# A cross network kernel: set-up reordered under manual scheduling, and chunk 0's h1 made while M is under way, its samples' halves side by side in the output columns

## The chip, the cores and the metric

One core of one Trainium2 chip. The time is the device time of one execution in microseconds (us); medians of several executions on the same chip are given. All arithmetic is fp32. A span is the profiled execution's length on the core, about 2 us shorter than that execution's time.

## The reference

A compressed interaction network of three layers on x of shape (1024, 64, 16): samples, fields, embedding.

```python
x0 = h = x
for i in range(3):                                   # each W: (128, 64 * fields of h)
    z = einsum('bfe,bge->bfge', x0, h).reshape(Bn, f0 * fh, e)
    y = einsum('oc,bce->boe', Ws[i], z) + bs[i][None, :, None]
    x_i, h = (y[:, :64], y[:, 64:]) if i != 2 else (y, y)
    xs.append(x_i)
return concatenate(xs, 1).sum(2) @ fc_w.T + fc_b     # (1024, 1)
```

What goes only into the last dot product can be folded into weights ahead of it. The kernel makes three 64 x 64 matrices: v0, v1 and v2, in which fc_w's parts are multiplied into W0, W1 and W2, and from v2 and W1 a tensor M. Per sample column, what remains is: h1 (64 weight columns from W0 against all products of two fields), p (64 columns from M and v1 against the same products), the products of h1 with p, and y = v0 x, times x, all summed.

## The kernel before

32 samples and 16 embedding places make a chunk of 512 columns; there are 32 chunks. Products of fields are made by VectorE in four pieces `z` a chunk (128 x 2048), TensorE contracts them against 17 tiles of `w_all`, 128 columns wide: 64 for h1, 64 for p. Every second chunk, `y` is made with the block-diagonal `bd` (v0 twice).

```python
zp = tc.tile_pool(name="zp", bufs=3)                 # z
ps = tc.tile_pool(name="ps", bufs=2, space=PSUM)
...
for k in range(32):                                  # v2: one column each
    nc.tensor.matmul(pv2[:, k:k+1], w2s[:, k, :], fc2, start=True, stop=True)
... # copies to v2t; pm = v2t x w1s -> m_sb (M); m_sb -> md (DRAM), five writes
... # md -> ms1, ms2 and w_all[0:64, NT, 64:128], skewed, eleven reads
... # rows v1, v0: 8 matmuls with fc01 (two columns), then DMA to w_all and bd

def products(c, j):
    z = zp.tile([128, NI, N], F32, tag="z", name="z")
    nc.vector.tensor_tensor(z, xas[c], xbs[c][:, j, :]..., ALU.mult)
    for i in range(NI):
        t = j * NI + i
        nc.tensor.matmul(accs[c], w_all[:, t, :], z[:, i, :], start=(t == 0), stop=False)

def combine(c):
    ... # q <- acc[64:128] (ScalarE); uu <- (acc[0:64] + bh1) * q (VectorE)
    if half == 0:
        return
    y = ps.tile([128, N], F32, tag="y", name=f"y_{c}", bufs=1)
    nc.tensor.matmul(y, bd, xxs[c // 2], start=True, stop=True)
    nc.vector.scalar_tensor_tensor(uu[:, 1, :], y, cx, xxs[c // 2], ALU.add, ALU.mult)
    nc.vector.tensor_reduce(acc[:, :, c // 2, :], uu..., AX.X, ALU.add)

for c in range(NCH + 1):
    if c + 1 < NCH: load_chunk(c + 1)
    if c < NCH:
        accs[c] = ...; products(c, 0); products(c, 1)
    if c > 0: combine(c - 1)
    if c < NCH:
        products(c, 2); products(c, 3); squares(c)
```

In this kernel the program order of the source is not the order that is built: a scheduler places instructions.

## Time and profile before

| | before |
|---|---|
| time, median (lowest to highest) | 552.89 us (551.77 to 554.76), 3 runs |
| profiled span (an execution of 556.77 us) | 555.0 us |
| set-up, until the first full matmul of chunk 0 | 66.3 us |
| a pair of chunks in the loop | 30.04 us |
| tail behind the last matmul of the loop | 8.7 us |

In the groups below (busy us, mean ns, then idle time before them), the main matmul never waits.

```profile
L236 PE MATMUL acc<-z,w_all 128*128 128x512 f32 x1024 | 447.2, 592 | 0.0
```

So only the set-up and the tail leave room.

### The profile page before, as it was taken

How to read it: one execution, taken by the hardware profiler on the slowest of the kernel's cores; microseconds unless marked ns; L12 is line 12 of the kernel's file. 1: busy time of each engine (PE TensorE's matmuls, PEld its weight loads, DVE VectorE, ACT ScalarE, POOL GpSimd, SP SyncE). 2: the span in 40 equal slices, each digit the busy share in tenths (PEclk: the TensorE clock that was granted, in tenths of full speed). 3: DMA queues.
4: the chain of work that ended last, by engine and by line, in shares of the span. 5: the costliest groups of instructions: out<-in, count | busy, mean ns of one | idle time of the engine just before them, and what ended most of it. 6: DMA issues, size and time to landing. Idle time of an engine off the chain costs nothing.

```text
span 555.0 us, 3402 instructions
## 1 busy us (share of the span) xinstructions
PE 515.9 (93%) x1240; PEld 231.9 (42%) x1240; DVE 352.0 (63%) x205; ACT 44.9 (8%) x81; POOL 5.3 (1%) x18
## 2 busy tenths in 40 slices
PE   5803799999999999999999999999999999999997
PEld 5600144444444444444444444444444444444442
DVE  0250076768677677768676867767776867686751
ACT  0100300000000000000000000000000000000001
POOL 3000000000000000000000000000000000000000
PEclk9967699999999999999999999999999999999999
DMA  8999998787777777877778777777787877874000
GB/s 254 185 283 210 205 208 170 144 163 146 156 153 159 150 152 162 180 161 161 160 147 165 146 154 154 154 150 154 161 180 161 165 155 151 162 152 77 0 1 0
DMA packets 33114, 85.33 MB, mean 154 GB/s; under 512 B 6405, under 2 KB 6949, under 8 KB 28710
## 3 DMA queue, kind: packets, MB, share of 16 engines
q1 hardware_dynamic: 29234, 81.84, 71.1%
q10 hardware_dynamic: 3608, 3.28, 2.8%
q8 instruction: 10, 0.16, 0.2%
q14 instruction: 6, 0.05, 0.0%
q0 software_dynamic: 256, 0.00, 0.0%
HBM read 82.89 MB, written 2.17 MB: 153 GB/s over the span
## 4 chain that ended last, share of the span: by engine, by line
PE 92%; DMA 6%; DVE 0%; ACT 0%; issue 0%; ACTq 0%; SPq 0%
PE acc L236 79%; PE acc L240 5%; DMA w<-in_wv 3%; PE pv L133 2%; PE y L254 2%; PE pv L197 2%; DMA ms<-md 1%; DMA fc<-in_fc_w 1%; DMA md<-m_sb 1%; PE pm L146 1%; PE po L281 0%; DVE acc L256 0%; DVE uu L255 0%; ACT res L289 0%; ACT q L249 0%
## 5 line engine op out<-in xcount | busy, mean ns | idle before, releaser
L236 PE MATMUL acc<-z,w_all 128*128 128x512 f32 x1024 | 447.2, 592 | 0.0
L231 DVE TENSOR_TENSOR z<-xa,xb 128x2048 f32<-128x2048 f32 x128 | 293.3, 2292 | 135.9 <-PE acc L236 134.6
L236 PEld LDWEIGHTS acc<-z,w_all 128*128 128x128 f32 x1024 | 194.5, 190 | 244.5 <-issue 244.4
L249 ACT COPY q<-acc 64x512 f32<-64x512 f32 x32 | 18.6, 582 | 443.8 <-PE acc L240 443.8
L197 PE MATMUL pv<-w,fc 128*2 128x512 f32 x16 | 11.5, 887 | 27.9 <-DMA w<-in_wv 14.9
L240 PE MATMUL acc<-zl,w_all 128*128 128x512 f32 x64 | 32.7, 592 | 0.0
L250 DVE SCALAR_TENSOR_TENSOR uu<-acc,bh,q 64x512 f32<-64x512 f32 x32 | 23.7, 740 | 10.0 <-ACT q L249 9.5
L239 ACT ACTIVATE zl<-xa 64x512 f32<-64x512 f32 x32 | 20.1, 628 | 3.6 <-DMA xa<-in_x 3.6
L133 PE MATMUL pv<-fc,w2s 128*128 128x1 f32 x64 | 13.8, 352 | 6.6 <-DMA fc<-in_fc_w 6.6
L256 DVE TENSOR_REDUCE acc<-uu 128x64 f32<-128x1024 f32 x16 | 19.5, 1220 | 0.5
L240 PEld LDWEIGHTS acc<-zl,w_all 128*128 128x128 f32 x64 | 12.2, 190 | 15.3 <-issue 15.3
L197 PEld LDWEIGHTS pv<-w,fc 128*2 128x2 f32 x16 | 1.6, 108 | 37.6 <-issue 21.5
L133 PEld LDWEIGHTS pv<-fc,w2s 128*128 128x128 f32 x64 | 13.7, 332 | 6.6 <-DMA fc<-in_fc_w 6.6
L254 PE MATMUL y<-xx,bd 128*128 128x512 f32 x32 | 16.3, 592 | 0.0
L136 DVE COPY v2t<-pv 64x32 f32<-64x32 f32 x2 | 0.4, 184 | 20.4 <-PE pv L133 20.4
L255 DVE SCALAR_TENSOR_TENSOR uu<-y,cx,xx 128x512 f32<-128x512 f32 x16 | 11.9, 745 | 0.0
L188 DVE TENSOR_TENSOR w_all<-ms,ms 128x1024 f32<-128x1024 f32 x1 | 1.2, 1224 | 13.2 <-DMA ms<-md 13.2
L254 PEld LDWEIGHTS y<-xx,bd 128*128 128x128 f32 x32 | 6.1, 190 | 7.7 <-issue 7.7
L199 ACT COPY vrow<-pv 2x512 f32<-2x512 f32 x8 | 4.2, 570 | 33.3 <-DMA ms<-md 32.2
L184 DVE MEMSET ms<- 64x64 f32 x1 | 0.1, 112 | 9.7 <-DMA ms<-md 9.7
L146 PE MATMUL pm<-w1s,v2t 64*64 64x512 f32 x16 | 5.6, 809 | 0.5 <-DVE v2t L137 0.5
L152 DVE COPY m_sb<-pm 64x512 f32<-64x512 f32 x4 | 2.7, 683 | 3.2 <-PE pm L146 3.2
(33 smaller groups left out, 21.0 us busy)
## 6 DMA issues: line engine op xcount, KB each, us to landing
xa<-in_x SPq DMA_DIRECT2D x64, 512.0 KB, 5.8
xb<-in_x SPq DMA_DIRECT2D x64, 512.0 KB, 7.1
zl<-in_x SPq DMA_DIRECT2D x32, 128.0 KB, 4.2
xx<-in_x SPq DMA_DIRECT2D x32, 128.0 KB, 4.1
w2s<-in_wv SPq DMA_DIRECT2D x4, 512.0 KB, 7.8
w<-in_wv SPq DMA_DIRECT2D x4, 512.0 KB, 11.9
w1s<-in_w1h SPq DMA_DIRECT2D x1, 1024.0 KB, 13.4
md<-m_sb ACTq DMA_DIRECT2D x2, 512.0 KB, 7.1
```

Source lines behind the costliest of these rows:

```text
L133: nc.tensor.matmul(pv2[:, k : k + 1], w2s[:, k, :], fc2, start=True, stop=True)
L146: nc.tensor.matmul(pm, v2t[to], w1s[to, m * 512 : (m + 1) * 512], start=True, stop=True)
L197: nc.tensor.matmul(pv, fc01, w01[:, m * 512 : (m + 1) * 512], start=True, stop=True)
L231: nc.vector.tensor_tensor(z, xas[c], xbs[c][:, j, :].unsqueeze(1).to_broadcast([128, NI, N]), ALU.mult)
L236: nc.tensor.matmul(accs[c], w_all[:, t, :], z[:, i, :], start=(t == 0), stop=False)
L239: nc.scalar.activation(zls[c][0:64], xas[c][0:64, 0, :], AF.Square)
L240: nc.tensor.matmul(accs[c], w_all[:, NT, :], zls[c], start=False, stop=True)
L249: nc.scalar.copy(q, accs[c][64:128])
L250: nc.vector.scalar_tensor_tensor(uu[to, 0, :], accs[c][0:64], bh1, q, ALU.add, ALU.mult)
L254: nc.tensor.matmul(y, bd, xxs[c // 2], start=True, stop=True)
L255: nc.vector.scalar_tensor_tensor(uu[:, 1, :], y, cx, xxs[c // 2], ALU.add, ALU.mult)
L256: nc.vector.tensor_reduce(acc[:, :, c // 2, :], uu.rearrange("p k (b e) -> p k b e", e=E), AX.X, ALU.add)
```

## The change

The intent: shorten the 66 us before the loop. Chunk 0's h1 (`ph`) needs only W0, so it can be made while M goes through DRAM; p (`pq`) follows when M is there. Each has 64 weight columns, half of the main matmul's 128, and one of 64 columns takes as long as one of 128. So the 512 samples are split: the first 256 go to output partitions 0 to 63 and the others to 64 to 127, two matmuls side by side. v2 is made as rows, v0 is postponed to chunk 2, and the writes of md are cut in seven. To hold the order the scheduler is turned off. The diff, cut to what matters:

```diff
+    ctx.enter_context(tc.manual_schedule())
-    zp = tc.tile_pool(name="zp", bufs=3)
+    zp = tc.tile_pool(name="zp", bufs=7)
-    ps = ... bufs=2
+    ps = ... bufs=4
 # v2
-    for k in range(32):
-        nc.tensor.matmul(pv2[:, k : k + 1], w2s[:, k, :], fc2, start=True, stop=True)
-    ... tensor_copy(v2t[to, ...], pv2[...])
+    for k in range(2):
+        for m in range(4):
+            nc.tensor.matmul(pv, fc2, w2s[k][:, cols], start=True, stop=True)
+            ... copy to vrow[0:1, cols], VectorE and ScalarE by turns
+        ... two nc.scalar.dma_start(out=v2t[...], in_=vrow[0:1, :]...)
 # md: seven writes; the last overlaps the sixth
+    nc.scalar.dma_start(out=md[64:96, 64:68, :], in_=m_lo[0:32, 0:4, :])
+    nc.scalar.dma_start(out=md[64:68, 64:96, :], in_=m_lo[0:4])
+    nc.scalar.copy(xas[0][F:128], xas[0][0:F])     # upper half of chunk 0
 # chunk 0
+    zs = [product(0, 0)]
+    first_weights()
+    zs += [product(0, j) for j in range(1, NJ)]
+    load_chunk(1)
+    def side_by_side(p, part, tiles):
+        cols = slice(part * F, (part + 1) * F)
+        for t in tiles:
+            for n in range(2):
+                nc.tensor.matmul(p[halves[n]], w_all[:, t, cols],
+                                 z[:, n * H2 : (n + 1) * H2], ...)
+    side_by_side(ph, 0, range(NT + 1))
+    second_weights()
+    constants()
+    side_by_side(pq, 1, range(NT))
+    v_row("v1", fc1, wx1, [w_all[64:128, NT, 64:128]])
+    load_chunk(2)
 # loop
-    for c in range(NCH + 1):
+    for c in range(1, NCH + 1):
+        if c + 2 < NCH: load_chunk(c + 2)
         products(c, 0); products(c, 1)
-        if c > 0: combine(c - 1)
+        if c == 1: side_by_side(pq, 1, [NT]); ...   # finish chunk 0
+        else: factors(c - 1)                        # q, uu
+        if c == 2: v_row("v0", fc0, wx0, [bd[to, to] for to in halves])
+        if c % 2 == 0: sums(c // 2 - 1)             # y, y's step, the sum
         products(c, 2); products(c, 3); squares(c)
```

More of the change, by code (lines that the diff above doesn't have):

```diff
@@ L44, in cin_kernel @@
 @with_exitstack
-def cin_kernel(ctx, tc, x2, w0a, w0b, w1h, wv2, wv01, b0, b1, b2, fc_w, fc_b, out):
+def cin_kernel(ctx, tc, x2, w0a, w0b, w1h, wv2, wx1, wx0, b0, b1, b2, fc_w, fc_b, out):
     nc = tc.nc
+    ctx.enter_context(tc.manual_schedule())
     const = ctx.enter_context(tc.tile_pool(name="const", bufs=1))
-    setup = ctx.enter_context(tc.tile_pool(name="setup", bufs=2))
     xp = ctx.enter_context(tc.tile_pool(name="xp", bufs=3))
-    zp = ctx.enter_context(tc.tile_pool(name="zp", bufs=3))
+    zp = ctx.enter_context(tc.tile_pool(name="zp", bufs=7))
     sp = ctx.enter_context(tc.tile_pool(name="sp", bufs=2))
-    ps = ctx.enter_context(tc.tile_pool(name="ps", bufs=2, space=bass.MemoryType.PSUM))
+    ps = ctx.enter_context(tc.tile_pool(name="ps", bufs=4, space=bass.MemoryType.PSUM))
     dr = ctx.enter_context(tc.tile_pool(name="dr", bufs=1, space=bass.MemoryType.DRAM))
@@ L61, in rows, with big, load_chunk @@
         )
-    fc01 = const.tile([128, 2], F32, tag="fc01", name="fc01")
+    def big(name):
+        return zp.tile([128, NI * N], F32, tag="z", name=name)
+    halves = [slice(0, F), slice(F, 128)]
+    w2s = [big(f"w2_{k}") for k in range(2)]
+    w1s = big("w1s")
     fc2 = const.tile([128, 1], F32, tag="fc2", name="fc2")
-    nc.gpsimd.memset(fc01, 0.0)
     nc.scalar.dma_start(out=fc2, in_=fc_w[0, 128:256].unsqueeze(1))
-    nc.scalar.dma_start(out=fc01[0:64, 0:1], in_=fc_w[0, 0:64].unsqueeze(1))
-    nc.scalar.dma_start(out=fc01[64:128, 1:2], in_=fc_w[0, 64:128].unsqueeze(1))
-    bh1 = const.tile([F, 1], F32, tag="bh1", name="bh1")
+    for k in range(4):
+        cols = slice(k % 2 * 1024, (k % 2 + 1) * 1024)
+        nc.sync.dma_start(out=w2s[k // 2][:, cols], in_=wv2[:, k * 1024 : (k + 1) * 1024])
+    nc.sync.dma_start(out=w1s, in_=w1h)
+    xas, xbs, zls, xxs = {}, {}, {}, {}
+    def load_chunk(c, mirror=False):
+        xa = xp.tile([128, NI, N], F32, tag="xa", name=f"xa_{c}")
+        xb = xp.tile([128, NJ, N], F32, tag="xb", name=f"xb_{c}")
+        zl = xp.tile([128, N], F32, tag="zl", name=f"zl_{c}")
+        for half in range(2):
+            to = halves[half]
+            if half == 0 or not mirror:
+                nc.sync.dma_start(out=xa[to], in_=rows(c, 0, [[1, NI]]))
+            nc.sync.dma_start(out=xb[to], in_=rows(c, 16 * half + 4, [[4, NJ]]))
+        nc.sync.dma_start(out=zl[F:128], in_=rows(c, 0, []))
+        if c % 2 == 0:
+            xxs[c // 2] = sp.tile([128, N], F32, tag="xx", name=f"xx_{c}", bufs=3)
+        nc.sync.dma_start(out=xxs[c // 2][halves[c % 2]], in_=rows(c, 0, []))
+        xas[c], xbs[c], zls[c] = xa, xb, zl
+    fc1 = const.tile([128, 1], F32, tag="fc1", name="fc1")
+    fc0 = const.tile([128, 1], F32, tag="fc0", name="fc0")
+    bh1 = const.tile([128, 1], F32, tag="bh1", name="bh1")
     bh2 = const.tile([F, 1], F32, tag="bh2", name="bh2")
@@ L76, in cin_kernel @@
     b1c = b1.unsqueeze(1)
-    nc.gpsimd.dma_start(out=bh1, in_=b0c[64:128])
+    for to in halves:
+        nc.gpsimd.dma_start(out=bh1[to], in_=b0c[64:128])
+        nc.gpsimd.dma_start(out=fc1[to], in_=fc_w[0, 64:128].unsqueeze(1))
+        nc.gpsimd.dma_start(out=fc0[to], in_=fc_w[0, 0:64].unsqueeze(1))
     nc.gpsimd.dma_start(out=bh2, in_=b1c[64:128])
@@ L97, in cin_kernel @@
     nc.gpsimd.memset(bd, 0.0)
-    w2s = const.tile([128, 32, 128], F32, tag="w2s", name="w2s")
-    w1s = const.tile([128, 32 * F], F32, tag="w1s", name="w1s")
     w0t = const.tile([128, NT + 1, F], F32, tag="w0t", name="w0t")
     w0u = const.tile([128, NT, F], F32, tag="w0u", name="w0u")
-    for k in range(4):
-        nc.sync.dma_start(out=w2s[:, 8 * k : 8 * k + 8, :], in_=wv2[:, 8 * k : 8 * k + 8, :])
-    nc.sync.dma_start(out=w1s, in_=w1h)
-    xas, xbs, zls, xxs = {}, {}, {}, {}
-    def load_chunk(c):
-        xa = xp.tile([128, NI, N], F32, tag="xa", name=f"xa_{c}")
-        xb = xp.tile([128, NJ, N], F32, tag="xb", name=f"xb_{c}")
-        zl = xp.tile([128, N], F32, tag="zl", name=f"zl_{c}")
-        for half in range(2):
-            to = slice(half * F, (half + 1) * F)
-            nc.sync.dma_start(out=xa[to], in_=rows(c, 0, [[1, NI]]))
-            nc.sync.dma_start(out=xb[to], in_=rows(c, 16 * half + 4, [[4, NJ]]))
-        nc.sync.dma_start(out=zl[F:128], in_=rows(c, 0, []))
-        if c % 2 == 0:
-            xxs[c // 2] = sp.tile([128, N], F32, tag="xx", name=f"xx_{c}")
-        to = slice(c % 2 * F, (c % 2 + 1) * F)
-        nc.sync.dma_start(out=xxs[c // 2][to], in_=rows(c, 0, []))
-        xas[c], xbs[c], zls[c] = xa, xb, zl
-    load_chunk(0)
+    load_chunk(0, mirror=True)
     nc.sync.dma_start(out=w0t, in_=w0a)
@@ L130, in cin_kernel @@
     v2t = const.tile([128, F], F32, tag="v2t", name="v2t")
-    pv2 = ps.tile([128, 32], F32, tag="set", name="pv2", bufs=4)
-    for k in range(32):
-        nc.tensor.matmul(pv2[:, k : k + 1], w2s[:, k, :], fc2, start=True, stop=True)
-    for half in range(2):
-        to = slice(half * F, (half + 1) * F)
-        nc.vector.tensor_copy(v2t[to, 0:32], pv2[0:64])
-        nc.vector.tensor_copy(v2t[to, 32:64], pv2[64:128])
-    m_sb = const.tile([F, F, F], F32, tag="m_sb", name="m_sb")
+    for k in range(2):
+        vrow = big(f"v2row_{k}")
+        for m in range(4):
+            cols = slice(m * 512, (m + 1) * 512)
+            pv = ps.tile([1, 512], F32, tag="set", name=f"pv2_{k}_{m}")
+            nc.tensor.matmul(pv, fc2, w2s[k][:, cols], start=True, stop=True)
+            if m % 2:
+                nc.vector.tensor_copy(vrow[0:1, cols], pv)
+            else:
+                nc.scalar.copy(vrow[0:1, cols], pv)
+        for half in range(2):
+            nc.scalar.dma_start(
+                out=v2t[half * F + k * 32 : half * F + (k + 1) * 32],
+                in_=vrow[0:1, :].rearrange("p (o f) -> p o f", f=F),
+            )
@@ L142, in cin_kernel @@
+    md = dr.tile([EXT, EXT, F], F32, tag="md", name="md")
+    m_sb = [big(f"m_{k}") for k in range(2)]
     for m in range(4):
         for half in range(2):
-            to = slice(half * F, (half + 1) * F)
-            pm = ps.tile([F, 512], F32, tag="set", name=f"pm_{m}_{half}", bufs=4)
-            nc.tensor.matmul(
-                pm, v2t[to], w1s[to, m * 512 : (m + 1) * 512], start=True, stop=True
-            )
-            f0 = half * 32 + m * 8
-            m_to = m_sb[:, f0 : f0 + 8, :].rearrange("p f g -> p (f g)")
+            to = halves[half]
+            pm = ps.tile([F, 512], F32, tag="set", name=f"pm_{m}_{half}")
+            cols = slice(m * 512, (m + 1) * 512)
+            nc.tensor.matmul(pm, v2t[to], w1s[to, cols], start=True, stop=True)
@@ L151, in cin_kernel @@
             if half:
-                nc.vector.tensor_copy(m_to, pm)
+                nc.vector.tensor_copy(m_sb[half][0:F, cols], pm)
             else:
-                nc.scalar.copy(m_to, pm)
-    md = dr.tile([EXT, EXT, F], F32, tag="md", name="md")
-    nc.scalar.dma_start(out=md[0:64, 0:64, :], in_=m_sb)
-    nc.scalar.dma_start(out=md[64:96, 0:64, :], in_=m_sb[0:32])
-    nc.scalar.dma_start(out=md[0:64, 64:96, :], in_=m_sb[:, 0:32, :])
-    nc.scalar.dma_start(out=md[64:96, 64:68, :], in_=m_sb[0:32, 0:4, :])
@@ L160, in cin_kernel @@
-    nc.scalar.dma_start(out=md[64:68, 64:96, :], in_=m_sb[0:4, 0:32, :])
+                nc.scalar.copy(m_sb[half][0:F, cols], pm)
+    m_lo, m_hi = [m[0:F].rearrange("p (f g) -> p f g", g=F) for m in m_sb]
+    nc.scalar.dma_start(out=md[0:64, 0:32, :], in_=m_lo)
+    nc.scalar.dma_start(out=md[0:64, 32:64, :], in_=m_hi)
+    nc.scalar.dma_start(out=md[64:96, 0:32, :], in_=m_lo[0:32])
+    nc.scalar.dma_start(out=md[64:96, 32:64, :], in_=m_hi[0:32])
+    nc.scalar.dma_start(out=md[0:64, 64:96, :], in_=m_lo)
@@ L161, in cin_kernel @@
+    nc.scalar.dma_start(out=md[64:96, 64:68, :], in_=m_lo[0:32, 0:4, :])
+    nc.scalar.dma_start(out=md[64:68, 64:96, :], in_=m_lo[0:4])
+    nc.scalar.copy(xas[0][F:128], xas[0][0:F])
+    nc.scalar.activation(zls[0][0:64], xas[0][0:64, 0, :], AF.Square)
     ms1 = const.tile([128, NT, F], F32, tag="ms1", name="ms1")
@@ L170, in cin_kernel @@
     for half in range(2):
-        to = slice(half * F, (half + 1) * F)
+        to = halves[half]
         b = 16 * half + 4
@@ L177, in cin_kernel @@
         for i in range(NI):
-            nc.scalar.dma_start(
+            (nc.scalar if i % 2 else nc.sync).dma_start(
                 out=ms2[to].rearrange("p (j i) g -> p j i g", i=NI)[:, :, i, :],
@@ L182, in cin_kernel @@
     nc.scalar.dma_start(out=w_all[0:64, NT, 64:128], in_=skewed(0, [[1, F]]))
-    nc.vector.memset(ms2[64:128, 3 * NI, :], 0.0)
-    nc.vector.memset(w0u[64:128, 3 * NI, :], 0.0)
-    nc.vector.tensor_tensor(w_all[:, 0:NT, 0:64], w0t[:, 0:NT, :], w0u, ALU.add)
-    nc.vector.tensor_copy(w_all[0:64, NT, 0:64], w0t[0:64, NT, :])
-    nc.vector.tensor_tensor(w_all[:, 0:NT, 64:128], ms1, ms2, ALU.add)
-    vrow = const.tile([2, F * F], F32, tag="vrow", name="vrow")
-    for k in range(4):
-        w01 = setup.tile([128, 1024], F32, tag="w01", name=f"w01_{k}")
-        nc.sync.dma_start(out=w01, in_=wv01[:, k * 1024 : (k + 1) * 1024])
-        for m in range(2):
-            pv = ps.tile([2, 512], F32, tag="set", name=f"pv_{k}_{m}", bufs=4)
-            nc.tensor.matmul(pv, fc01, w01[:, m * 512 : (m + 1) * 512], start=True, stop=True)
-            col = (2 * k + m) * 512
-            nc.scalar.copy(vrow[:, col : col + 512], pv)
@@ L200, in cin_kernel @@
-    nc.scalar.dma_start(
-        out=w_all[64:128, NT, 64:128], in_=vrow[1:2, :].rearrange("o (f g) -> o f g", g=F)
-    )
-    for half in range(2):
-        to = slice(half * F, (half + 1) * F)
-        nc.scalar.dma_start(
-            out=bd[to, to], in_=vrow[0:1, :].rearrange("o (f g) -> o f g", g=F)
-        )
-    cx = const.tile([128, 1], F32, tag="cx", name="cx")
-    pcx = ps.tile([128, 1], F32, tag="set", name="pcx", bufs=4)
-    for half in range(2):
-        nc.tensor.matmul(
-            pcx[half * F : (half + 1) * F], v2t[0:64], bh2, start=True, stop=True
-        )
@@ L216, in cin_kernel, with first_weights @@
-    nc.scalar.copy(cx, pcx)
-    cst = const.tile([1, 1], F32, tag="cst", name="cst")
-    pc = ps.tile([1, 1], F32, tag="set", name="pc", bufs=4)
-    for j in range(2):
-        nc.tensor.matmul(
-            pc, fcol[:, j : j + 1], bcol[:, j : j + 1], start=(j == 0), stop=(j == 1)
-        )
-    nc.scalar.activation(cst, pc, AF.Identity, bias=fcb, scale=float(E))
+    def first_weights():
+        nc.vector.memset(w0u[64:128, 3 * NI, :], 0.0)
+        nc.vector.tensor_tensor(w_all[:, 0:NT, 0:64], w0t[:, 0:NT, :], w0u, ALU.add)
+        nc.vector.tensor_copy(w_all[0:64, NT, 0:64], w0t[0:64, NT, :])
@@ new lines, in second_weights, with v_row @@
+    def second_weights():
+        nc.vector.memset(ms2[64:128, 3 * NI, :], 0.0)
+        nc.vector.tensor_tensor(w_all[:, 0:NT, 64:128], ms1, ms2, ALU.add)
+    def v_row(name, fc, wx, outs):
+        w = big(f"w_{name}")
+        nc.sync.dma_start(out=w, in_=wx)
+        vrow = sp.tile([128, NI * N], F32, tag="vrow", name=f"vrow_{name}", bufs=1)
+        for half in range(2):
+            for m in range(4):
+                cols = slice(m * 512, (m + 1) * 512)
+                pv = ps.tile([1, 512], F32, tag="set", name=f"pv_{name}_{half}_{m}")
+                nc.tensor.matmul(pv, fc[halves[half]], w[halves[half], cols], start=True, stop=True)
+                nc.scalar.copy(vrow[half * F : half * F + 1, cols], pv)
+        for to in outs:
+            for half in range(2):
+                nc.scalar.dma_start(
+                    out=to[half * 32 : (half + 1) * 32],
+                    in_=vrow[half * F : half * F + 1, :].rearrange("p (f g) -> p f g", g=F),
+                )
@@ L226, in cin_kernel, with new_acc, product @@
     acc = const.tile([128, 2, NCH // 2, CB], F32, tag="acc", name="acc")
     accs, uus = {}, {}
-    def products(c, j):
-        z = zp.tile([128, NI, N], F32, tag="z", name="z")
+    def new_acc(c):
+        accs[c] = ps.tile([128, N], F32, tag="acc", name=f"acc_{c}", bufs=3)
+    def product(c, j):
+        z = zp.tile([128, NI, N], F32, tag="z", name=f"z_{c}_{j}")
         nc.vector.tensor_tensor(
@@ L233, in products, with contract @@
         )
+        return z
+    def contract(c, j, z):
         for i in range(NI):
@@ L236, in products, with square, factors @@
             nc.tensor.matmul(accs[c], w_all[:, t, :], z[:, i, :], start=(t == 0), stop=False)
+    def products(c, j):
+        contract(c, j, product(c, j))
+    def square(c):
+        nc.scalar.activation(zls[c][0:64], xas[c][0:64, 0, :], AF.Square)
     def squares(c):
-        nc.scalar.activation(zls[c][0:64], xas[c][0:64, 0, :], AF.Square)
+        square(c)
         nc.tensor.matmul(accs[c], w_all[:, NT, :], zls[c], start=False, stop=True)
-    def combine(c):
-        half = c % 2
-        to = slice(half * F, (half + 1) * F)
-        if half == 0:
+    def factors(c):
+        to = halves[c % 2]
+        if c % 2 == 0:
@@ L246, in combine @@
             uus[c // 2] = sp.tile([128, 2, N], F32, tag="uu", name=f"uu_{c}")
-        uu = uus[c // 2]
         q = sp.tile([F, N], F32, tag="q", name=f"q_{c}")
         nc.scalar.copy(q, accs[c][64:128])
-        nc.vector.scalar_tensor_tensor(uu[to, 0, :], accs[c][0:64], bh1, q, ALU.add, ALU.mult)
-        if half == 0:
-            return
-        y = ps.tile([128, N], F32, tag="y", name=f"y_{c}", bufs=1)
-        nc.tensor.matmul(y, bd, xxs[c // 2], start=True, stop=True)
-        nc.vector.scalar_tensor_tensor(uu[:, 1, :], y, cx, xxs[c // 2], ALU.add, ALU.mult)
+        nc.vector.scalar_tensor_tensor(
+            uus[c // 2][to, 0, :], accs[c][0:64], bh1[0:64], q, ALU.add, ALU.mult
+        )
@@ L256, in combine, with sums @@
+    def sums(k):
+        y = ps.tile([128, N], F32, tag="y", name=f"y_{k}", bufs=1)
+        nc.tensor.matmul(y, bd, xxs[k], start=True, stop=True)
+        nc.vector.scalar_tensor_tensor(uus[k][:, 1, :], y, cx, xxs[k], ALU.add, ALU.mult)
         nc.vector.tensor_reduce(
-            acc[:, :, c // 2, :], uu.rearrange("p k (b e) -> p k b e", e=E), AX.X, ALU.add
+            acc[:, :, k, :], uus[k].rearrange("p k (b e) -> p k b e", e=E), AX.X, ALU.add
         )
-    for c in range(NCH + 1):
-        if c + 1 < NCH:
-            load_chunk(c + 1)
+    cx = const.tile([128, 1], F32, tag="cx", name="cx")
@@ new lines, in cin_kernel, with constants @@
+    cst = const.tile([1, 1], F32, tag="cst", name="cst")
+    def constants():
+        pcx = ps.tile([128, 1], F32, tag="set", name="pcx")
+        for half in range(2):
+            nc.tensor.matmul(
+                pcx[half * F : (half + 1) * F], v2t[0:64], bh2, start=True, stop=True
+            )
+        nc.scalar.copy(cx, pcx)
+        pc = ps.tile([1, 1], F32, tag="set", name="pc")
+        for j in range(2):
+            nc.tensor.matmul(
+                pc, fcol[:, j : j + 1], bcol[:, j : j + 1], start=(j == 0), stop=(j == 1)
+            )
+        nc.scalar.activation(cst, pc, AF.Identity, bias=fcb, scale=float(E))
@@ new lines, in cin_kernel @@
+    zs = [product(0, 0)]
+    first_weights()
+    zs += [product(0, j) for j in range(1, NJ)]
+    load_chunk(1)
+    H2 = N // 2
+    def side_by_side(p, part, tiles):
+        cols = slice(part * F, (part + 1) * F)
+        for t in tiles:
+            z = zls[0] if t == NT else zs[t // NI][:, t % NI, :]
+            for n in range(2):
+                nc.tensor.matmul(
+                    p[halves[n]], w_all[:, t, cols], z[:, n * H2 : (n + 1) * H2],
+                    start=(t == 0), stop=(t == NT),
+                )
@@ L263, in cin_kernel @@
+    ph = ps.tile([128, H2], F32, tag="acc", name="ph", bufs=3)
+    pq = ps.tile([128, H2], F32, tag="acc", name="pq", bufs=3)
+    side_by_side(ph, 0, range(NT + 1))
[5 more added lines that the diff above has]
+    for c in range(1, NCH + 1):
+        if c + 2 < NCH:
+            load_chunk(c + 2)
         if c < NCH:
-            accs[c] = ps.tile([128, N], F32, tag="acc", name=f"acc_{c}")
+            new_acc(c)
@@ L265, in cin_kernel @@
             products(c, 0)
             products(c, 1)
-        if c > 0:
-            combine(c - 1)
+        if c == 1:
+            side_by_side(pq, 1, [NT])
+            q0 = sp.tile([128, H2], F32, tag="q", name="q_0")
+            nc.scalar.copy(q0, pq)
+            uus[0] = sp.tile([128, 2, N], F32, tag="uu", name="uu_0")
+            for n in range(2):
+                at = halves[n]
+                nc.vector.scalar_tensor_tensor(
+                    uus[0][0:64, 0, n * H2 : (n + 1) * H2], ph[at], bh1[at], q0[at],
+                    ALU.add, ALU.mult,
+                )
+        else:
+            factors(c - 1)
@@ L269, in cin_kernel @@
+        if c == 2:
+            v_row("v0", fc0, wx0, [bd[to, to] for to in halves])
+        if c % 2 == 0:
+            sums(c // 2 - 1)
         if c < NCH:
@@ L276, in cin_kernel @@
     for k in range(2):
-        po = ps.tile([1, 2, half_pairs * CB], F32, tag="set", name=f"po_{k}", bufs=4)
+        po = ps.tile([1, 2, half_pairs * CB], F32, tag="set", name=f"po_{k}")
         pairs = slice(k * half_pairs, (k + 1) * half_pairs)
@@ L320 @@
         "w1h": w1[64:].reshape(64, 2, 32 * F).transpose(1, 0, 2).reshape(128, 32 * F),
-        "wv2": w2.reshape(128, 2, 32, F).transpose(0, 2, 1, 3).reshape(128, 32, 128),
-        "wv01": np.concatenate([w0[:64], w1[:64]], axis=0).reshape(128, F * F),
+        "wv2": w2.transpose(0, 2, 1).reshape(128, F * F),
+        "wx1": w1[:64].reshape(64, 2, 32 * F).transpose(1, 0, 2).reshape(128, 32 * F),
+        "wx0": w0[:64].reshape(64, 2, 32 * F).transpose(1, 0, 2).reshape(128, 32 * F),
         "b0": np.asarray(L0_rec_b0),
```

## The prediction

> **What bounds the kernel now.** I read the page's span and engine table first, then the chain that ended last in order of time, then the timeline of one pair of chunks.

> ```profile
> span 555.0 us, 3402 instructions
> ...
> PE 515.9 (93%) x1240; PEld 231.9 (42%) x1240; DVE 352.0 (63%) x205; ACT 44.9 (8%) x81; POOL 5.3 (1%) x18
> ```

> ```profile
> 20.85 3.58 PE pm L146 x7
> ...
> 29.36 11.91 DMA w<-in_wv
> ...
> 52.26 6.73 DMA ms<-md
> ...
> 59.61 6.33 PE pv L197 x8
> ...
> 66.32 13.93 PE acc L236 x32
> 80.25 0.86 PE acc L240 x2
> ...
> 102.57 0.86 PE y L254 x2
> ...
> 545.47 0.87 PE acc L240 x2
> ```

> The second fence has pieces of the chain (start, duration, what). From 66.3 us to 546.3 TensorE never waits: a chunk is 34 records (17 fp32 matmuls of two records each), 13.73 + 0.86 = 14.59 us, and every second chunk has one y matmul more, 0.86 us. Check: 66.3 + 32 x 14.59 + 15 x 0.86 = 546.1. Ahead lie 66 us of set-up, behind it 8.7 us of tail. The change is aimed at the 66 us. There the way to M (v2, pm, md to DRAM, skewed ms reads back) ends about 63, and the pv rows about 66.

> What makes the steady part free of waits is the order on VectorE. One pair in the timeline (weight loads and SyncE rows left out):

> ```profile
> 159.25 2.29 DVE L231 TENSOR_TENSOR z<-xa,xb 128x2048 f32<-128x2048 f32 x1 [1.22 <-PE acc L236]
> ...
> 162.49 1.02 PE L254 MATMUL y<-xx,bd 128*128 128x512 f32 x2
> 162.69 2.29 DVE L231 TENSOR_TENSOR z<-xa,xb 128x2048 f32<-128x2048 f32 x1 [1.14 <-PE acc L236]
> ...
> 164.90 0.74 DVE L255 SCALAR_TENSOR_TENSOR uu<-y,cx,xx 128x512 f32<-128x512 f32 x1
> ...
> 165.68 1.22 DVE L256 TENSOR_REDUCE acc<-uu 128x64 f32<-128x1024 f32 x1
> ...
> 166.98 2.29 DVE L231 TENSOR_TENSOR z<-xa,xb 128x2048 f32<-128x2048 f32 x1
> ```

> Columns: start, duration, engine, line. In the source y's matmul, its two VectorE steps and then products 2 and 3 follow one another. The scheduler did not keep that. In the built order VectorE makes this chunk's four products and one of the next chunk before it turns to y. So when TensorE has passed y it finds its next operand ready.

> [...] The trace agrees as far as it goes: all its rows are in built order. So the built order of the changed kernel decides. [...] The trace agrees: the last pm ends at 26.5 and the granted clock is half from 31.0 (4.5 us later); after 46.6 it falls at 51.5.

> ```profile
> 30.00:31.00 1.00, 0.00 (x0) 0.00 (x0) 1.00 (x1) 0.00 (x0) 0.00 (x0) 1.00 1.34 279
> 31.00:32.00 1.00, 0.00 (x0) 0.00 (x0) 1.00 (x3) 0.00 (x0) 0.00 (x0) 0.51 1.00 258
> ```

> (The clock is the third number from the right.) [...] No trace here has column pairs. The nearest, pm, whose halves lie in different row groups, took 5.6 us for 16 records, 0.35 each against 0.43 alone: a modest overlap. So I give side-by-side pairs 55%.

> **The change part by part.** The built order has, on every engine, the program order of the source.

> *v2.* Removed: 32 one-column matmuls (64 records, 13.8 us, 6.6 to 20.4). Added: 8 matmuls of 512 columns, 8 x 0.86 = 6.9 us, so done at about 13.5 (the last w2s landed at about 11.2). But the row must then be spread over partitions by DMA: copy 0.7, issue 0.6, landing 6.6 as bd<-vrow took: v2t at about 21.3. Before it was ready at 21.2. Nothing gained, and TensorE has idled 7.7 us, so pm starts at half clock: some 2.5 us worse. M is in SBUF at about 30 instead of 27.2.

> *md.* The same 2 MB, in seven writes. The sixth and the last overlap, so the last waits for the sixth to land, behind 2 MB (about 38), and its own issue took 2.3 us before, landing 4.4: about 42.5 against 38.5.

> *Chunk 0.* The mirror copy of xa stands on ScalarE behind all md issues, so it runs at about 40.3 to 42.2 (2048 columns at 0.58 us per 512, less fixed cost). The first product waits for it: 44.5; first weights 1.5; three products 6.9, to 53; ms add 1.2, to 54. The eleven ms reads have 42.8 to 53 to land, with fewer large loads beside them than before; I expect that to do. ph follows the products and ends about 56. pq: 16 tiles x 4 records of 256 columns at 0.215 us: 13.8 us one by one, 6.9 in pairs: ends at 63 (pairs).

> *v1, then chunk 1.* 8 matmuls, 6.9: 70. Products 0 and 1: 6.9. The last tile of pq waits for the v1 row (copy 0.6, two issues, landing 6.6, about 78): 1.3 us. Then product 2 of chunk 1 stands on VectorE behind uu, which needs pq: copy 0.4, two uu of 0.4, product 2.3: 3.7 us. Chunk 1 ends about 90.

> *Chunk 2.* w_v0 loads late (about 2.5 us), v0 6.9, then y waits for bd: copy 0.6, four issues 2.4[...]: 6 us. Then a y wait as below, 4.5. Chunk 2 ends about 125. Before it ended at 111.1: **+14 us**, +29 without pairs; weighted +20.

> *Every even chunk from 4 to 30.* VectorE now has, in this order, products 0 and 1, uu, the y step, the sum, product 2, product 3. TensorE has y after product 1's tiles. With 0 at the chunk's first matmul: y's records issue at 6.87 and 7.30, end 7.89; y step 0.74, to 8.68; sum 1.22, to 9.93; product 2 2.29, to 12.24; TensorE goes on at 12.29, where it could have at 7.73. **4.55 us, 14 times: +64 us.** Seven z buffers do not help, since order, not room, holds product 2 back. Odd chunks do not wait: product 2 is ready 4 us after uu can start, before 6.9.

> *Clock.* The gap without matmuls is 4.4 us. [...] Estimate: 14 x 0.29 x 2 = **+8 us**.

> *Tail.* Same steps: 0. Sum: 20 + 64 + 8 = 92 on a median of 552.9: **645 us**.

> **The rivals.** (a) *Set-up gain*: no y wait matters, half of chunk 0 hidden, quieter DMA queues shorten M. Speaking for it: that is the intent, and ms reads took 24 us (38.6 to 63). Without y waits and clock loss, I would get 553 + 14 = 567; if md and ms came 10 us earlier than I think as well, 557; with a better overlap at bd and v1, some 548. Against it: the built order, which no DMA timing can mend. (b) *No column pairs*: ph and pq take 14 us each: 653. (c) [...] 14 x 1.7 to 3 us in place of 8: 660 to 680. (d) *VectorE becomes the bound*: four products, uu, half of y and sum are 11 us a chunk against 14.6. No.

> **Range and chances.** The y wait is arithmetic on durations that hardly vary (64, plus or minus 5). Set-up is plus or minus 12, clock 0 to 25 above. 80% range 622 to 668. Chances: faster 0.03, within 2% 0.03, slower 0.94; the 0.06 is for a mistake in reading the order.

> **What would show it.** VectorE's y step (TensorE's y as releaser) idles about 6 us in even chunks; TensorE's L248 idles about 4.5 us, 14 times, behind product z; even chunks last 20 us, odd ones 14.6. v2t lands near 21, md near 42, ph begins near 46, pq ends near 63 (78 without pairs); y_0 waits some 6 us on bd. Half clock shows after some y waits only. I am wrong if TensorE runs through the even chunks, or if the first full chunk starts before 55.

## More of the kernel before

The page's slices give each engine's busy share in tenths for 40 equal stretches. `PEclk` is the clock that TensorE was granted.

```profile
PE   5803799999999999999999999999999999999997
...
PEclk9967699999999999999999999999999999999999
```

Behind the fifth slice TensorE is full and at full clock.

## The result

A ratio is the mean time of one kernel's fast runs over that of the other's fast runs of the same rounds, so it is not quite the ratio of the medians.

| | before | after |
|---|---|---|
| median (lowest to highest), 4 runs each | 553.03 us (551.77 to 554.76) | 685.37 us (684.23 to 686.7) |
| ratio, 95% interval | | 1.2391 (1.235 to 1.2432) |
| chunk 3 begins, in the profile | 111.15 us | 135.40 us |
| a pair of chunks in the loop | 30.04 us | 37.5 us |
| behind the last matmul of the loop | 8.7 us | 8.4 us |

The changed kernel is 132 us slower. It is slower as predicted, and yet 17 us above the top of the range. Its page answers to the lines of before:

```profile
span 683.3 us, 3499 instructions
...
PE 566.0 (83%) x1310; PEld 240.2 (35%) x1310; DVE 345.8 (51%) x206; ACT 53.8 (8%) x94; POOL 7.8 (1%) x22
...
PE   5327876797979797997979797979979797979797
...
PEclk9659978798989899898989898998989898989989
...
L248 PE MATMUL acc<-z,w_all 128*128 128x512 f32 x992 | 480.2, 643 | 68.3 <-DVE z L240 68.3
```

Two things are new in the loop: TensorE is full only in every second slice, and the clock falls in every second slice. In the last line the matmul waits 68.3 us for z from VectorE (0.0 before), and one takes 643 ns in the mean (592 before). TensorE's busy time rose by 50 us although it has no more to do (e1_y_last, with the same work, has 523.0 us): most of that is the clock. One pair of chunks in the timeline (start, duration, engine, line; weight loads left out):

```profile
306.20 1.02 PE L274 MATMUL y<-xx,bd 128*128 128x512 f32 x2
...
307.26 0.75 DVE L275 SCALAR_TENSOR_TENSOR uu<-y,cx,xx 128x512 f32<-128x512 f32 x1 [6.37 <-PE y L274]
308.05 1.22 DVE L276 TENSOR_REDUCE acc<-uu 128x64 f32<-128x1024 f32 x1
309.18 8.89 DVE L240 TENSOR_TENSOR z<-xa,xb 128x2048 f32<-128x2048 f32 x4
...
311.52 10.05 PE L248 MATMUL acc<-z,w_all 128*128 128x512 f32 x16 [4.29 <-DVE z L240]
```

Compare with the pair in the prediction. There VectorE made its products first and had to turn to y only afterwards. Here it waits 6.37 us for y with nothing to do, then does y's step and the sum, and only then the product for which TensorE waits. TensorE's 16 records then take 10.05 us; at full clock 7.13 (e2_warm). The clock around this gap (the number third from the right):

```profile
309.00:310.00 1.00, 0.00 (x0) 0.00 (x0) 1.00 (x2) 0.00 (x0) 0.00 (x0) 1.00 0.00 0
310.00:311.00 1.00, 0.00 (x0) 0.00 (x0) 1.00 (x1) 0.00 (x0) 0.00 (x0) 0.80 0.00 0
311.00:312.00 1.00, 0.48 (x1) 0.48 (x2) 1.00 (x2) 0.00 (x0) 0.00 (x0) 0.50 0.00 0
...
317.00:318.00 1.00, 1.00 (x4) 0.35 (x3) 1.00 (x1) 0.00 (x0) 0.00 (x0) 0.79 0.75 141
```

```profile
156.86 0.87 PE y L274 x2
...
194.05 0.87 PE y L274 x2
...
231.41 0.87 PE y L274 x2
...
268.87 0.87 PE y L274 x2
...
306.36 0.87 PE y L274 x2
...
343.89 0.87 PE y L274 x2
...
381.42 0.87 PE y L274 x2
```

The differences are 37.19, 37.36, 37.46, 37.49, 37.53, 37.53, and then they stay at 37.54 us, which is 11 x 3.413. Each is half as far from 37.54 as the one before (0.35, 0.18, 0.08, 0.05, 0.01). The clock's falls are 37.55 us apart in the mean, 11 windows, from the first of the 14 (160.41) to the last (648.52); the starts of y came to this period by and by. The pairs have locked to the windows.

The whole, summed from the chain: chunk 3 begins at 135.40 (24.3 later than before); 29 chunks at 14.59 and 14 y at 0.86 are 435.1; the last chunk ends at 674.93, so 104.4 us are lost in the loop, 14 x 7.46.

### The profile page after: what moved, and what is told of

Its sections match the earlier page's. It is cut to its first block, busy times and chain, and to the rows that moved or that the text cites. A ratio compares the mean times of both kernels' runs of the same rounds, so it can differ in the third digit from the quotient of the medians.

```text
span 683.3 us, 3499 instructions
## 1 busy us (share of the span) xinstructions
PE 566.0 (83%) x1310; PEld 240.2 (35%) x1310; DVE 345.8 (51%) x206; ACT 53.8 (8%) x94; POOL 7.8 (1%) x22
## 4 chain that ended last, share of the span: by engine, by line
PE 77%; DMA 10%; DVE 8%; issue 3%; ACTq 1%; ACT 1%; SPq 0%; DVEq 0%
PE acc L248 68%; DVE z L240 5%; PE acc L258 4%; DMA xa<-in_x 4%; DMA ms<-md 2%; PE y L274 2%; DVE uu L275 2%; PE pv L144 1%; DMA md<-m 1%; DMA w_v<-in_wx 1%; DMA v2t<-v2row 1%; PE pm L164 1%; DMA fc<-in_fc_w 1%; PE pv_v L222 1%; ACTq L173 0%
## 5 line engine op out<-in xcount | busy, mean ns | idle before, releaser
L248 PE MATMUL acc<-z,w_all 128*128 128x512 f32 x992 | 480.2, 643 | 68.3 <-DVE z L240 68.3
L248 PEld LDWEIGHTS acc<-z,w_all 128*128 128x128 f32 x992 | 203.9, 208 | 340.5 <-issue 251.3
L240 DVE TENSOR_TENSOR z<-xa,xb 128x2048 f32<-128x2048 f32 x128 | 284.5, 2280 | 15.5 <-ACT xa L178 14.6
L311 PE MATMUL ph<-z,w_all 128*64 128x256 f32 x64 | 8.9, 447 | 19.1 <-DVE w_all L206 19.1
L254 ACT ACTIVATE zl<-xa 64x512 f32<-64x512 f32 x31 | 19.5, 628 | 1.9 <-DMA bd<-vrow_v 1.9
L144 PE MATMUL pv<-w,fc 128*1 128x512 f32 x16 | 9.2, 736 | 5.9 <-DMA fc<-in_fc_w 5.9
L311 PEld LDWEIGHTS ph<-z,w_all 128*64 128x64 f32 x64 | 5.3, 164 | 23.1 <-DVE w_all L206 19.9
L311 PE MATMUL pq<-z,w_all 128*64 128x256 f32 x64 | 8.8, 441 | 4.2 <-DVE w_all L211 4.2
L222 PE MATMUL pv_v<-w_v,fc 64*1 64x512 f32 x32 | 10.6, 588 | 1.2 <-DMA w_v<-in_wx 1.2
L223 ACT COPY vrow_v<-pv_v 1x512 f32<-1x512 f32 x16 | 8.6, 572 | 24.0 <-PE pv_v L222 23.9
L146 DVE COPY v2row<-pv 1x512 f32<-1x512 f32 x4 | 2.7, 679 | 13.2 <-PE pv L144 13.2
## 6 DMA issues: line engine op xcount, KB each, us to landing
w_v<-in_wx SPq DMA_DIRECT2D x2, 1024.0 KB, 10.7
```

The lines of the kernel that those rows point to most:

```text
L144: nc.tensor.matmul(pv, fc2, w2s[k][:, cols], start=True, stop=True)
L222: nc.tensor.matmul(pv, fc[halves[half]], w[halves[half], cols], start=True, stop=True)
L240: nc.vector.tensor_tensor(z, xas[c], xbs[c][:, j, :].unsqueeze(1).to_broadcast([128, NI, N]), ALU.mult)
L254: nc.scalar.activation(zls[c][0:64], xas[c][0:64, 0, :], AF.Square)
L311: nc.tensor.matmul(p[halves[n]], w_all[:, t, cols], z[:, n * H2 : (n + 1) * H2], start=(t == 0), stop=(t == NT),)
```

## The experiments

Each kernel was correct. Ratios are to the kernel before, in the same rounds; the sets ran on three chips, on which its medians were 552.8 to 554.2 us. All runs were fast ones but one of e4_scheduler.

### The order on VectorE: e1_y_last

The changed kernel with y's step and the sum behind products 2 and 3 on VectorE; TensorE's order is the same.

```diff
-        if c % 2 == 0: sums(c // 2 - 1)
+        if c % 2 == 0: y = y_mm(c // 2 - 1)         # TensorE alone
         products(c, 2); products(c, 3); squares(c)
+        if c % 2 == 0: y_step(c // 2 - 1, y); y_sum(c // 2 - 1)
```

> Only VectorE's order in even chunks is changed: y's step and the sum come after products 2 and 3; TensorE's order stays. Theory (order is the whole steady loss, wait 4.5 us and half clock 3 us in each of 14 pairs): pairs last 30.1 us again, nothing falls to half clock after 135 us, time about 685 - 104 = 581 us. Rival (the half clock comes from elsewhere[...] and only the wait goes): 685 - 64 = 621 us with half clock still there. If the set-up loss of 24 us is as read, the ratio to before is about 1.05.

575.31 us (574.43 to 576.31), ratio 1.0387 (1.0363 to 1.0411). 110 us come back from moving two instructions per pair. (The profiled spans differ by 108.8 us: 104.4 in the loop and 4.4 in chunk 2, where y's step stood first as well.)

```profile
span 574.5 us, 3499 instructions
...
PE   5407777869999999999999999999999999999997
...
PEclk9766797879999999999999999999999999999999
```

The loop is full, at full clock, and its pairs take 30.04 us as before. So the whole loss in the loop comes from this order; neither the seven z buffers nor transfers have a part in it. What stays, 21 us against before's 554.2 on that chip, is set-up.

### Waiting and clock apart: e2_warm

Five useless matmuls, 4.3 us of work, behind y in the 14 even chunks.

```diff
+        if c % 2 == 0 and 2 < c < NCH:
+            for _ in range(5):
+                nc.tensor.matmul(junk, bd, w_all[:, 0:4, :]..., start=True, stop=True)
```

> The order of the changed kernel is kept; TensorE is given five useless 512-column matmuls (4.3 us) behind y in each of the 14 even chunks, into a bank nobody reads. Theory (the 3 us above the wait are the clock, lost because TensorE is idle): the wait is filled, the granted clock stays 1.0, pairs last 34.6 us, time about 685 - 14 x 2.9 = 644 us: more work, less time. Rival (the clock is not the cause, the records after the wait are slow for another reason, such as VectorE's products coming at 2.29 us): 685 us or a little more.

644.06 us (643.46 to 646.6), ratio 1.1636 (1.1604 to 1.1669). With 60 us of work added, the changed kernel gets 41 us faster.

```profile
PE 585.0 (91%) x1450; PEld 251.7 (39%) x1450; DVE 345.8 (54%) x206; ACT 53.8 (8%) x94; POOL 7.8 (1%) x22
...
PEclk9758879699999999999999999999999999999999
...
297.65 8.89 DVE L240 TENSOR_TENSOR z<-xa,xb 128x2048 f32<-128x2048 f32 x4
299.99 7.13 PE L248 MATMUL acc<-z,w_all 128*128 128x512 f32 x16
```

TensorE's product 2 comes no earlier (5.16 us after the start of y in the chains of both kernels), but its 16 records take 7.13 us in place of 10.05, the clock stays up, and a pair takes 34.6 us. This splits the 7.46 us of a pair: 4.56 waiting (34.60 - 30.04), 2.9 clock. In the whole kernel: 64 us of waiting and 41 of clock.

### A shorter gap: e3_sum_later

Only the sum is moved behind product 2; y's step stays ahead of it.

> Only the sum (1.22 us) is moved, to behind product 2; y's step still stands before product 2. Theory [...]: the gap is 4.3 - 1.2 = 3.1 us[...]; pairs last 30.0 + 3.3 = 33.3 us; time about 685 - 14 x 4.2 = 626 us. Rival (any gap makes TensorE slow afterwards, in proportion): only the 1.2 us go, 14 times: 668 us.

646.64 us (642.43 to 649.78), ratio 1.1669 (1.1605 to 1.1734): neither of the two. The gap shrank to 3.04 us, and the 626 us were reckoned with a clock that holds, which was the author's estimate. In the trace it still falls in 10 of the 14 pairs, and from 262 to 568 us in every second one:

```profile
330.00:331.00 1.00, 0.81 (x2) 0.00 (x0) 0.15 (x1) 0.00 (x0) 0.00 (x0) 1.00 0.00 0
331.00:332.00 1.00, 0.00 (x0) 0.00 (x0) 1.00 (x2) 0.00 (x0) 0.00 (x0) 1.00 0.00 0
332.00:333.00 1.00, 0.00 (x0) 0.00 (x0) 1.00 (x1) 0.00 (x0) 0.00 (x0) 1.00 0.00 0
333.00:334.00 1.00, 0.15 (x1) 0.15 (x1) 1.00 (x2) 0.00 (x0) 0.00 (x0) 0.74 0.00 0
...
336.00:337.00 1.00, 1.00 (x2) 0.39 (x2) 1.00 (x1) 0.00 (x0) 0.00 (x0) 0.55 0.00 0
```

It fell at 333.48, so the window before began at 330.07, and in that TensorE worked until 330.82: 22% of the window. The fall came behind a window that was not empty. The next gap lies otherwise in its windows: 43% and 68% are busy, and the clock holds. Here the pairs take 33.35 and 34.88 us by turns, together 68.2, 20 windows: locked again. (There is a trace of one run only; the four runs lie 7 us apart and may have fallen into other patterns.) The half clock lasts one window here (to 336.9); TensorE is back 0.4 us into it and busy for 89% of it.

### The lock: e5_lock

One useless matmul of 256 columns (0.43 us) in each of 14 odd chunks, where TensorE does not wait.

> The changed kernel with one useless 256-column matmul (0.43 us of TensorE time) in each of the 14 odd chunks from 5 on, in a stretch where TensorE does not wait. Theory (pairs have locked to the clock windows: their period has converged to 37.54 us = 11 x 3.413 us, because warming up ends on a fixed grid): the 0.43 us are taken out of the half-speed stretch and the period stays 37.54; time 685 us, plus at most 1. Rival (the agreement with 11 windows is chance; a pair simply costs wait plus a fixed penalty): 685 + 14 x 0.43 = 691 us, period 37.97.

685.14 us (682.74 to 687.3), ratio 1.2376 (1.2328 to 1.2424). Fourteen times 0.43 us of work on the critical engine cost nothing. The pairs in its chain of waits:

```profile
266.43 0.87 PE y L274 x2
...
303.97 0.87 PE y L274 x2
...
341.51 0.87 PE y L274 x2
```

37.54 us, constant. An estimate from these times gives the reason. Let s be the time from the clock's fall to TensorE's restart. The half clock lasts 6.83 us in each of the changed kernel's 14 pairs, so 6.83 - s of it is spent working at half speed, and half of that is lost. A pair takes 34.60 + (6.83 - s)/2. If it takes longer than the 11 windows by which the falls lie apart, the next restart comes later behind its fall by the excess d, s grows by d, and the next pair is d/2 shorter. So deviations halve, as the times above did. The point of rest is s = 0.95; the trace of the changed kernel has 311.52 - 310.6 = 0.9. For e5_lock it is s = 1.81, and its trace has 1.74.

### What counts as busy: e8_warm_narrow and e9_warm_two

e2_warm with its five matmuls one weight column wide (`bd[:, 0:1]`), and with two in place of five.

> e2_warm with its five useless matmuls made one weight column wide in place of 128. They take TensorE as long (512 columns of samples each), but fill one column of the array. Theory A (the clock goes by the time in which TensorE has a matmul under way): as e2_warm, 644 us, pairs of 34.6, no half clock in the loop. Theory B (it goes by how much of the array works; hint: in f1 a window of 3.4 us that was some 96% busy with one-column matmuls did not bring the clock up): the clock falls as in the changed kernel, pairs 37 or more, 680 us or more.

> e2_warm with two useless matmuls in place of five: 1.73 us of the 4.4 us gap are filled, 2.6 us stay without a matmul, so that a window of 3.41 us is at the least 24% busy. In e3_sum_later a window 22% busy brought the clock down, one 43% busy did not. If the limit is under 24%: no half clock in the loop, pairs of 34.6, 644 us. If it is above 24%: the pairs step by 34.6 - 10 x 3.413 = 0.5 us through the windows, so that some of them fall: between 646 and 665 us by where between 24 and 43% it lies.

e8_warm_narrow: 644.98 us (644.46 to 645.73), ratio 1.1655 (1.1638 to 1.1673), the same as e2_warm, with no half clock in the loop (PEclk 9 in each of its slices, 7.06 to 7.07 us for the 16 records behind the useless matmuls). Five of these with one weight column kept the clock up as well as five with 128. The hint from f1 that stands in the expectation must have another cause: there matmuls with one weight column on 64 rows kept TensorE busy from 38.69 us on, and the clock rose only at 45.6. Whether the 64 rows are it was not tried.

e9_warm_two: 651.47 us (648.73 to 652.64), ratio 1.1755 (1.1726 to 1.1784), within the 646 to 665 of a limit above 24%. Gaps are 2.58 us; in four of the 14 pairs the clock fell. The first:

```profile
195.00:196.00 1.00, 0.23 (x1) 0.00 (x0) 1.00 (x2) 0.00 (x0) 0.00 (x0) 1.00 0.00 0
...
199.00:200.00 1.00, 1.00 (x2) 0.33 (x1) 1.00 (x2) 0.00 (x0) 0.00 (x0) 0.60 0.00 0
```

It fell at 199.20. The window before, from 195.79, had TensorE idle until 197.82, so it was 41% busy. The other three falls came behind windows 36%, 31% and 39% busy. Behind windows 44%, 47% and more busy none came. In e3_sum_later a fall came behind one window 41% busy, and none behind others 41% to 43% busy. So in these two loops all falls came behind windows up to about 41% busy; the ends of matmuls are modelled in the profile, so the last digit is not safe. For the matmuls of the set-up this was not shown.

All 14 pairs of the changed kernel fell. The windows ahead of its falls were 21%, 11%, 6% and 3% busy in the first four, and 1% or less in the others. An estimate from the 41% above: wherever its gap of 4.29 us lies in the windows, one of them has at least half of it, 2.15 us, empty, and so is at most 37% busy. By this estimate no phase was safe: the lock sets what a fall costs, and not whether there is one.

### The order alone, by the scheduler: e4_scheduler

The changed kernel without its line `tc.manual_schedule()`.

> One line is undone: the manual schedule. The scheduler then orders all engines; the built order has products ahead of y's steps in even chunks, the v1 row in two halves around pq, the mirror copy ahead of the md writes and chunk 1's loads ahead of the ms reads. Theory: no y waits, so at most 581; the set-up is also a little shorter (mirror copy early, product 2 of chunk 1 no longer behind uu, bd hidden by products): 555 to 570 us. Rival (the new set-up itself costs 24 us whatever the order): about 580 us.

566.54 us (564.52 to 573.54, the highest being the slow run), ratio 1.021 (1.0181 to 1.0239); the verdict is unclear, and the profiled run was one of the slow state, so its trace is used for order alone. The scheduler again puts products ahead of y's step. One line of the change therefore costs about 119 us, and with the scheduler the rest of the change still gains nothing.

### The set-up: e6_bd_later and e7_x1_held

Both start from e1_y_last. e6_bd_later makes the first y in chunk 3 in place of chunk 2, where TensorE stands 4.3 us waiting for `bd`.

> On the version with y's steps last: the first y (pair 0) is made in chunk 3 instead of right behind the v0 rows in chunk 2, so that the bd transfer lies beside products. Theory: the wait for bd (4.3 us) and what half clock follows it (1 to 2 us) go: 575 - 6 = 569 us. Rival (bd's landing only moves to the next wait): 575 us.

569.2 us (568.73 to 569.87), ratio 1.0288 (1.0236 to 1.0341): the wait for bd was worth 6 us by the medians, as expected.

e7_x1_held holds back chunk 1's loads until the last read of M has landed, by a small write on the same queue that depends on it. In the changed kernel this read of 16 KB was issued at 49.76 and landed at about 60.1, while chunk 1's loads (from 45.65) kept the 16 DMA engines full (DMA share 1.12 and 1.05 from 50 to 55 and to 60.2); pq could begin only behind it.

> On the version with y's steps last: SyncE issues chunk 1's loads only after the last read of M has landed (a 16 KB copy of it to DRAM stands in front). Theory A (the reads of M come late only because chunk 1's 2.3 MB run beside them): pq starts at about 52 instead of 60.5; but chunk 1 then lands near 64 to 66, so at most 2 or 3 us of it reach the end: 572 to 576 us. Theory B (the transfers are at their limit in the set-up, whatever the order): chunk 1 and the v1 matrix come later by as much as M comes earlier, 575 to 582 us. Both have pq earlier; if pq is not earlier, contention is not what delays M.

578.72 us (578.17 to 579.91), ratio 1.0459 (1.0413 to 1.0506), no gain. M did land earlier: VectorE added M's parts at 55.0 (60.2 in the changed kernel) and pq ran straight behind ph, from 57.98. So the loads had been what held it back. But in the chain of waits of e7_x1_held what followed was:

```profile
57.32 15.35 DMA w_v<-in_wx
72.71 7.00 PE pv_v L222 x11
...
82.32 9.22 DMA w_all<-vrow_v
91.58 0.68 PE pq L318 x4
```

The v1 matrix now came late behind the held loads, and its row took 9.2 us to land. So the transfers as a whole, in this order, set the end; moving one moves the wait to another.

### Putting the parts together: f1, f2 and g_no_pairs

f1 has e1's order in the loop, v2 by 32 one-column matmuls again, the mirror copy ahead of md's writes, writes of md without overlap, both v matrices loaded early and their rows made while M is under way, M's reads on SyncE ahead of chunk 1's loads, pq whole before chunk 1, and nine z buffers.

> All together, aimed at a version that beats both: y's steps last; v2 by 32 one-column matmuls as before the change (no transfer, TensorE warm for pm); the mirror copy before the writes of M; these writes without overlap, so the last does not wait; both v matrices loaded before M is written and both v rows made while M is under way; reads of M ahead of chunk 1's loads; pq complete before chunk 1. Theory: pm ends at 27, M is written by 40, read by 50, pq ends 55 to 60 with nothing left over: 57 + 31 x 14.59 + 16 x 0.86 + 8.5 = 532 us, up to 545 if chunk 1's loads come late. Rival (the set-up is bound by transfers): no better than before, 553.

549.53 us (549.21 to 551.6), ratio 0.9937 (0.9892 to 0.9982): within 2% of before. Its trace shows why it gained no more: ScalarE, which copies the v rows, was issuing md's writes until 38; TensorE stood 7.1 us for the copies with ph behind them in its queue, and ph began only at 56.7.

```profile
38.69 8.71 PE L214 MATMUL pv_v<-w_v,fc 64*1 64x512 f32 x16 [7.11 <-ACT vrow_v L215]
```

f2 puts TensorE's work in another order and leaves v1's copies to VectorE. It also gives part of M's reads back to ScalarE and each v row a buffer of its own; the cut below leaves these out.

```diff
-    v_row("v1", ...); v_row("v0", ...)
-    side_by_side(ph, 0, range(NT + 1))
+    v_half("v1", fc1, w_v1, vrow1, 0, nc.vector.tensor_copy)
+    side_by_side(ph, 0, range(NT + 1))
+    v_half("v1", fc1, w_v1, vrow1, 1, nc.vector.tensor_copy)
+    v_half("v0", ..., 0, nc.scalar.copy); v_half("v0", ..., 1, nc.scalar.copy)
     constants(); second_weights()
     side_by_side(pq, 1, range(NT + 1))
```

> f1 with its set-up put in another order: TensorE makes the first half of v1, then ph, then the second half of v1, then v0, and last pq; nothing that waits for ScalarE stands between v2 and ph. Theory A (in f1 the set-up was lengthened by v rows that stalled 7 us behind ScalarE, which was issuing the stores of M, and by ph standing behind them): ph ends by about 40, pq runs 50 to 58, chunk 1 starts at 58 to 60, and the whole is 58.5 + 31 x 14.59 + 13.7 + 8.5 = 533 us, up to 542 if chunk 1's loads land late. Theory B (transfers bind the set-up however TensorE is ordered): chunk 1 starts near 70 as in f1, and the time is 547 to 552.

537.85 us (535.86 to 540.26), ratio 0.9733 (0.9694 to 0.9772): faster than before by 2.7%. TensorE's timeline in its set-up:

```profile
32.51 9.54 PE L307 MATMUL ph<-z,w_all 128*64 128x256 f32 x64
...
42.41 5.38 PE L212 MATMUL pv_v<-w_v,fc 64*1 64x512 f32 x16
48.33 3.59 PE L212 MATMUL pv_v<-w_v,fc 64*1 64x512 f32 x8 [0.54 <-ACT vrow L213]
...
52.23 7.13 PE L307 MATMUL pq<-z,w_all 128*64 128x256 f32 x64
...
59.96 14.00 PE L240 MATMUL acc<-z,w_all 128*128 128x512 f32 x32 [0.17 <-DVE z L232]
```

From 28 us on TensorE hardly waits: ph, the rows and pq fill the time in which M goes through DRAM. How much of the 12 us over f1 is due to TensorE's order and how much to the rest of the edit was not tried. Chunk 1 begins at 59.96, and 59.96 + 31 x 14.59 + 13.7 + 8.5 = 534.4, the span is 534.1.

g_no_pairs is f2 with ph and pq as plain matmuls, 64 weight columns by 512 samples.

```diff
-            for n in range(2):
-                nc.tensor.matmul(p[halves[n]], w_all[:, t, cols], z[:, n * H2 : (n + 1) * H2], ...)
+            nc.tensor.matmul(p, w_all[:, t, cols], z, ...)
```

> f2 with chunk 0's two products made without column pairs, one matmul of 64 weight columns by 512 columns of samples in place of two of 256 side by side. Theory A (the two halves do run at the same time, so pq takes about 7 us where one by one takes 64 x 0.215 = 13.8): f2 plus 6 to 8 us, as pq is on the path that starts chunk 1. Rival [...]: the time of f2 within 2 us.

546.71 us (546.52 to 552.7), ratio 0.9914 (0.9844 to 0.9984): 8.9 us above f2 by the medians, a little more than the 6 to 8 expected. In the profiled spans, 10.7 us apart, pq takes 6.8 us longer and begins 3.7 us later (55.97 against 52.23), behind a longer ph: ph is on the path as well.

```profile
55.97 13.95 PE L306 MATMUL pq<-z,w_all 128*64 128x512 f32 x32
```

13.95 us against 7.13 for the same arithmetic: the two halves do run at the same time here.

## Why the prediction was right or wrong

**Direction and its cause: right.** The prediction found the cause in the built order before anything ran: in even chunks VectorE turns to y before product 2. e1_y_last shows that this alone makes the loop's loss. The wait was put at 4.55 us, 14 times, 64 us; e2_warm measured 4.56.

**The clock: the term that failed.** The step that failed is "Estimate: 14 x 0.29 x 2 = **+8 us**". That 0.29 of the waits bring a fall, and that a fall costs 2 us, was the author's estimate and was not shown by a trace. It measured 41 us (the changed kernel less e2_warm): all 14 pairs fell, 2.9 us each, where "after some y waits only" was the sign given. This 33 us is the greater part of the 40 by which 685 exceeds 645. Three assumptions lay in it. (1) A gap was taken to bring the clock down in a share of 0.29; the gap of 4.29 us did in 14 of 14 pairs, one of 3.04 us in 10 (e3_sum_later) and one of 2.58 us in 4 (e9_warm_two). (2) Phases were taken as random; but pairs lock, so that one phase repeats and each fall costs the same (the constant 37.54 us, and e5_lock, where added work cost nothing). (3) The 2 us of a fall were too few; the half clock lasted 6.83 us in each pair, two windows, and cost 2.9. In the first of them, from 310.6, TensorE restarted at 311.52 and was busy for 73%, and the clock stayed down; behind 89% in e3_sum_later it rose. The rival (c), the clock biting at each wait, 660 to 680, was the right one, and it was given too little weight: the text named it, yet the range ends at 668, inside it. Its upper end for the clock, 14 x 3 us, is what was measured (41); the 685 lie above its 680 because the set-up cost 4 us more.

**Column pairs: right, but underrated.** They were given 55%; g_no_pairs shows that they work, 7.13 against 13.95 us. The prediction's 6.9 for pq stands. In the changed kernel pq's 64 records took 8.8 us, begun at half clock. The trace of before spoke more for pairs than the prediction read from it: pm's 0.35 us is a mean over two speeds. Its records last up to 1.11 us at first and 0.59 later, so the first half ran slow; the last eight start about 0.23 us apart (24.26 to 25.89), against 0.43 alone, which is nearly full overlap.

**Set-up: right in kind, +24.3 where pairs were to give +14.** Up to M in DRAM the steps hold: v2t was ready at 22.3 (predicted 21.3), md landed at 43.7 (42.5), ScalarE, whose seven issues of md's writes took 8.4 us, began its copy of chunk 0's half at 41.84 (40.3), ph ran from 47.6 to 56.9 (46 to 56). What failed is "the eleven ms reads have 42.8 to 53 to land; I expect that to do". The last landed at 60.1, and pq began at 61.5 in place of some 56. Then v1's rows ended at 75.5 (70), the row landed at 85.7 (78), pq's last tile waited 3.3 us (1.3). e7_x1_held shows that chunk 1's loads held M back; that they delayed v1's row as well is only likely. Chunk 1 ended at 101 (90), and chunk 2 at 135.4 (125). The bd wait was 4.3 us in the trace (6 predicted, half of it an estimate of bd's landing, which took 1.9) and worth 6 in e6_bd_later. Against the weighted +20 in the sum the miss is 4 us.

**Tail: right.** 8.4 us against 8.7.

The terms as measured: 24.3 + 64 + 41 - 0.3 = 129. The spans differ by 128.3 (683.3 - 555.0), the medians by 132, as the profiled execution of before, 556.77 us, was some 4 us longer than its median.

**Rival (a)**, a gain in set-up with no wait at y, was wrong for this kernel, but right as to what lay in the idea: f2 keeps ph, pq and their pairs, and gains 15 us.

## What to carry to other kernels

Where a scheduler is turned off, the order on every engine must be read again, above all on an engine that serves two purposes: the step that someone waits for goes first, the one that has time goes last. A gap on TensorE can cost more than its length, and in a loop of steady period the cost need not be a matter of chance: here a wait of 4.56 us cost 7.46 us with the half clock behind it, in pairs that settled at 37.54 us, 11 windows. Look at the granted clock behind each gap, and at whether the period is a whole number of the steps in which it changes. Work that fills a wait, such as a product whose weights are ready, pays only if nothing behind it in the queue is what the others wait for, so the same idea lost 21 us in one order of the set-up (e1_y_last) and won 15 in another (f2).
